# A two-layer graph kernel: some of layer 1's matrix products, its PSUM tiles, its decode buffers and one early sum are placed elsewhere in the order of work

## The chip, the core and the metric

The kernel runs on one core of a Trainium2 chip. The metric is the device time of one execution in microseconds (us). Three executions of the kernel before took 404.49, 404.73 and 406.21 us; the median, 404.73 us, is the time before. A separate execution was recorded by the hardware profiler. The engines are named as in the profile: PE is the matrix engine (PEld its weight loads), DVE the vector engine, ACT the activation engine, POOL the general engine, SP the queue that issues most DMAs.

## The reference, cut to what matters

There are 3327 nodes with 64 features and a dense 0/1 adjacency matrix. Layer 0 is a hyperbolic graph layer: for every pair of nodes a weight (a sigmoid of two logits) times a distance function of the two feature vectors, summed over the neighbours. Layer 1 gives each neighbour j of node i a weight 0.5 to the power of the number of neighbours behind it in the row, for the last 100 of them, and sums:

```python
h = relu(layernorm(x)); x = x + layer0(h, adj)      # pairs, sums over neighbours, then work per node
h = relu(layernorm(x)); support = h @ weight
rank = cumsum(adj != 0, axis=1)
k = minimum(rank[:, -1:], 100); pos = rank - (rank[:, -1:] - k)
w = mask * where(pos > 0, 0.5 ** (k - pos), 0)
x = x + w @ support + bias
```

Layer 1's weights depend on the adjacency alone, so they can be made while layer 0 runs. Its products need the new h of every node j, and so the end of layer 0 for that node.

## The kernel before, in words

**Tiles and rounds.** Nodes are padded to 26 blocks of 128. Columns i are cut into four strips of 8, 8, 6 and 4 blocks (`STRIPS`). Within a strip the row blocks j run from 25 down to 0. A round is one row block (strips 0 to 2) or two (strip 3), so there are 26, 26, 26 and 13 rounds, R = 91 of them, numbered n = 0 to 90. The loop `for n in range(2, R)` (L1228) issues them; rounds 0 and 1 are written out ahead of it.

**What a round does.** `load` brings the adjacency tile four rounds ahead. `edges` (L621, DVE) makes a 0/1 mask. `count` (L632 and L633, PE) adds masks into the PSUM tile `pc`, and `read` (L650 on ACT, L652 or L654 on DVE) takes out of `pc` the count for layer 1: as bytes into `behind_lo` and `behind_hi`, or, for the four row blocks 12 to 15 (`JD`), at once as ready bf16 weights into the tile `weight_of`. `products` (L678 and L679, PE) makes the pair terms in a tile `pq` of two PSUM banks, two buffers of it. `gelus` (L870, L871, ACT) works on `pq`, `sigmoids` (L661, ACT) makes `sg`, `pair_one` (L666, DVE) multiplies `sg` by the adjacency, and `pair_two` (L671, DVE) reads `pq` and multiplies. `total` (L691, PE) sums `sg` over j into PSUM banks `po0` and `po1`; it runs two rounds later. Counting runs one round ahead of the pairs.

**Order.** PE, DVE and ACT run their instructions in the order in which the code issues them, each one waiting at the head of its queue. In round 2 the order on PE is: products of round 3, count of round 3, sums of round 1 (`total(1)`, L1269). Then follow, in round 3, products of round 4 and count of round 4.

**End of a strip.** `strip_out` (L1172, DVE) copies the sums, `turn` (L1184, PE) transposes them, `per_node` copies the result (L1194, DVE) and starts `post`: some 60 small steps per node that end with `s2` (L1162 on ACT, L1164 on DVE), the operand of layer 1's products. `post` is a generator; each round lets it go on by some portions (`advance`). For the last strip its steps run on DVE, three powers on POOL, and three steps on ACT.

**Layer 1.** `order` holds row blocks 12 to 15, 0 to 11 and 16 to 21; 22 to 25 are `late`, since they need the last strip's `s2`. For each j, `add` issues 7 products (chunks n = 0 to 6 of the 3328 columns) into seven PSUM tiles `pw`. `decode` turns the bytes of a row block into weights: 22 blocks, on ACT one instruction (L1311), on DVE two (L1314, L1315). In order of their calls the 1st, 4th, 7th and so on go to ACT (`ACT_DECODES = 3`), 8 in all, and 14 to DVE. They go into 7 buffers `wt`. At step i of the loop over `order`, decoding has been issued for the first i + 5 entries (`LEAD = 4`), then `post` is advanced by 8 portions, then the seven products of order[i] are issued. After the loop the late blocks follow chunk by chunk (L1380), each chunk being copied out (L1358 to L1362) and multiplied by the layer's weight matrix (L1370).

All seven `pw` tiles come from a PSUM pool that is opened after every pool of layer 0 is closed (L1321 to L1323).

Of the kernel before, what the change touches and what calls it, by code (L numbers as in the profile page):

```python
# [2 lines left out]

# [1 line left out]

# [6 lines left out]
F32 = mybir.dt.float32  # L12
# [27 lines left out]
BIG, LATER, ACT = 4, 99, 100  # L40
ROUND = (3.5, 3.5, 2.8, 1.9)

LEAD = 4
ACT_DECODES = 3

GSTRIPS = [(0, 7), (7, 7), (14, 6), (20, 6)]
GFMAX = 7 * P
# [400 lines left out]
def fast(ctx, tc, x, adj_t, r, w_att, b_att, weight, bias, out, flag):  # L448
# [223 lines left out]

    def products(n):
        S = strips[rounds[n][0]]
        pq_of[n] = pq = ps.tile([P, FMAX], F32, name="pq", bufs=2)
        for j in js(n):
            for f0, f1 in S.hv:
                T.matmul(part(n, pq, j, f0, f1), ju[:KB, j, :], S.iu[:, f0:f1], start=True, stop=False)  # L678
                T.matmul(part(n, pq, j, f0, f1), jz[:, j, :], S.iz[:, f0:f1], start=False, stop=True)  # L679
# [13 lines left out]

    sums, pairs = ctx.enter_context(ExitStack()), ctx.enter_context(ExitStack())
    ps = sums.enter_context(tc.tile_pool(name="ps", bufs=1, space=PSUM))
    of_first = sums.enter_context(ExitStack())
    first_ps = of_first.enter_context(tc.tile_pool(name="first_ps", bufs=1, space=PSUM))
    strip = pairs.enter_context(tc.tile_pool(name="strip", bufs=2))
    work = pairs.enter_context(tc.tile_pool(name="work", bufs=2))
# [136 lines left out]
    edges(0)  # L836

    iz, iu = strip_in(0)
    pt = ps.tile([P, 16, P], F16, name="pq", bufs=2)
    for b in range(8):  # L840
        T.transpose(pt[:KB, b, :], nui[:, b, :], id16)
    pz = ps.tile([P, 16, P], F16, name="pq", bufs=2)
    for b in range(8):
        T.transpose(pz[:, b, :], nzi[:, b].rearrange("p c d -> p (c d)"), id16)
    for b in (0, 1):
# [4 lines left out]
    V.tensor_copy(ju[: KB + 7, last_j], pt[: KB + 7, 8:10, :])  # L850
    A.copy(iz, pz[:, :8, :])
    A.copy(jz[:, last_j], pz[:, 8:10, :])
    p3 = ps.tile([P, 16, P], F16, name="pq", bufs=2)
    for to, of in ((jz[:D], iz[D:]), (jz[D:], iz[:D]), (ju[:D], iu[:D]), (ju[D : D + 3], iu[D + 3 : D + 6]),
                   (ju[D + 3 : D + 6], iu[D : D + 3]), (ju[KB : KB + 7], iu[D:])):
        nc.gpsimd.dma_start(to[:, first_i], of)
# [64 lines left out]
    gelus(1)  # L921
    logits((high,))
    pair_one(1)
    p5 = ps.tile([P, FMAX], F32, name="pq", bufs=2)
    p4 = p5.bitcast(F16).rearrange("p (b q) -> p b q", q=P)
    turned_to(p4, low, 0)
    kept(p4, low, 0)
# [250 lines left out]

    def turn(k):
        nb = STRIPS[k][1]  # L1180
        pa = [bank(n) for n in range(nb // per_bank(k))]
        for b in range(nb):
            n, c0 = b // per_bank(k), b % per_bank(k) * (D + 1)
            T.transpose(pa[n][:, c0 : c0 + D + 1], strips[k].ot[:, b * P : (b + 1) * P], ident[: D + 1, : D + 1])  # L1184
        return pa
# [32 lines left out]
    def finish():  # L1218
# [2 lines left out]
                pass  # L1221
        stages.clear()

    stages, rest_of_ahead = [Stage(range_steps())], last_of_ahead()
    range_end = in_range()
    load(LOADS)
    load(LOADS + 1)
    for n in range(2, R):  # L1228
        k, lo, hi = rounds[n]
        m, w = n + AHEAD, span(n)  # L1230
        ended, turned = (n > i and rounds[n - i - 1][1] == 0 for i in (1, 2))
        if n + LOADS < R:
            if rounds[n + LOADS][2] == NB:
                strip_in(rounds[n + LOADS][0])
            load(n + LOADS)
        fresh = EARLY <= m < R
        two = fresh and len(js(m)) == 2
        if two:
            count(m, js(m)[0])
        apart = k + 1 == len(STRIPS)  # L1240
        if turned and not apart:
            pa = turn(k - 1)
        if n >= 4 and (apart or not turned):
            total(n - 2)
        gelus(n)
        asked_of_act()
        if turned and not apart:
            finish()
            stages.append(Stage(per_node(k - 1, pa)))
        pair_one(n)  # L1250
        if two:
            read(m, js(m)[0])
        if EARLY <= m + 1 < R:
            edges(m + 1)
        if n == 2:
            for j in js(2):
                read(2, j, True)
        if n < 4:
            products(n + 1)
        if fresh:  # L1260
            count(m, js(m)[-1])
        if n + 1 < R:
            sigmoids(n + 1)
        if fresh:
            read(m, js(m)[-1])
        if 4 <= n < R - 1:
            products(n + 1)
        if n == 2:
            total(1)  # L1269
        if ended:  # L1270
            strip_out(k - 1)
        if hi - lo > 1:
            advance(PORTIONS[k])
        if turned and apart:
            pa = turn(k - 1)
        pair_two(n)
        if turned and apart:
            finish()
            stages.append(Stage(per_node(k - 1, pa)))
        if n < 4:  # L1280
            next(rest_of_ahead)
            continue
        advance(PORTIONS[k])
        if turned and not apart:
            total(n - 2)
        if n > R - 3:
            next(range_end)
    total(R - 2)
    total(R - 1)
    strip_out(len(STRIPS) - 1)  # L1290
    pa = turn(len(STRIPS) - 1)
    pairs.close()


    late = STRIPS[-1][0]
    order = [*JD, *range(JD.start), *range(JD.stop, late)]
    chunks = [(q, r) for q in range(3) for r in range(2)] + [(3, None)]
    widths = [512] * 6 + [256]
    with tc.tile_pool(name="l1", bufs=2, reuse_waits="tile") as l1, tc.manual_schedule(engines=IN_ORDER):
        decoded = 0  # L1300

        def decode(j):

            nonlocal decoded
            if j in JD:
                return behind(j)
            wt = l1.tile([P, NP], U16, name="wt", bufs=7)
            decoded += 1
            to = by_parity(wt)
            if decoded % ACT_DECODES == 1:  # L1310
                A.activation(to, behind(j).rearrange("p (k r) -> p r k", r=2), AF.Copy, scale=128.0)  # L1311
            else:
                pairs_of = behind(j).bitcast(U16)
                V.tensor_scalar(to[:, 0], pairs_of, 0xFF, 7, op0=ALU.bitwise_and, op1=ALU.logical_shift_left)  # L1314
                V.tensor_scalar(to[:, 1], pairs_of, 0xFF00, 1, op0=ALU.bitwise_and, op1=ALU.logical_shift_right)  # L1315
            return wt
# [1 line left out]
        every = [*order, *range(late, NB)]  # L1318
        weights = {j: decode(j) for j in every[: len(JD) + 1]}
        stages.append(Stage(per_node(len(STRIPS) - 1, pa)))  # L1320
        sums.close()  # L1321
        l1_ps = ctx.enter_context(tc.tile_pool(name="l1_ps", bufs=1, space=PSUM, reuse_waits="tile"))
        pw = [l1_ps.tile([P, f], F32, name=f"pw{n}") for n, f in enumerate(widths)]  # L1323

        def add(j, wt, n):
            q, r = chunks[n]
            w = by_parity(wt.bitcast(BF16))[:, :, 512 * q : min(512 * q + 512, NP // 2)]
            T.matmul(pw[n], s2[:, j].rearrange("p c d -> p (c d)"), w if r is None else w[:, r],  # L1328
                     start=j == order[0], stop=j == NB - 1)

        def bias(b0, nb):
            xb = x_sb[:, b0 : b0 + nb]
# [2 lines left out]
        for i, j in enumerate(order):  # L1335
# [3 lines left out]
            asked_of_act()  # L1339
            advance(LAST)  # L1340
            for n in range(len(chunks)):
                add(j, weights[j], n)
            if i % 4 == 3 and i < STRIPS[-2][0]:
                bias(i - 3, 4)
        finish()
# [8 lines left out]
        def copied(n):  # L1354
            q, r = chunks[n]
            to = kept_of[q].rearrange("p (k r) -> p r k", r=2)
            if r is None:
                V.tensor_copy(to, by_parity(pw[n]))  # L1358
            elif r == 0:
                V.tensor_copy(to[:, 0], pw[n])  # L1360
            else:
                A.copy(to[:, 1], pw[n])  # L1362
# [75 lines left out]
```

## Time and profile before

| | us |
|---|---|
| median of three executions | 404.73 |
| the profiled execution, whole | 406.06 |
| its span from the first to the last instruction | 404.3 |
| DVE, ACT, PE busy in the span | 366.7, 355.8, 353.7 |
| POOL busy | 117.7 |
| layer 1's products, first to last of those in the loop | 354.11 to about 385.3 |

All times in the text are places in the profiled execution, counted from the start of its span, unless they are called the time or the median. The profiled execution is 1.76 us longer than its span, and 1.33 us longer than the median. A row of the timeline gives start, duration, engine, line, operation, output and inputs, and in brackets the idle time ahead of it with what ended it. The duration of a pipelined instruction reaches into that of the next one: a run of 138 products over 28.03 us gives one each 0.203 us, though each is written as some 0.36 us long.

### The profile page before, as it was taken

The numbers are of one execution on the slowest core, as the hardware profiler recorded it, in microseconds if no ns is written. First come the engines' busy times: TensorE is split into PE (matmuls) and PEld (weight loads), VectorE is DVE, ScalarE is ACT, GpSimd is POOL, SyncE is SP. The second block draws the span as 40 slices with busy tenths as digits, with TensorE's granted clock in tenths as the row PEclk, the third lists the DMA queues.
The fourth block names the chain that finished last, engine by engine and source line by source line (L and its number), as shares of the span: only waits on it lengthen the run. The fifth ranks groups of instructions, "written<-read, shape, count | busy, mean of one in ns | idle before, by whom it ended". The sixth has DMA issues, their size and how long they took to land.

```text
span 404.3 us, 4738 instructions
## 1 busy us (share of the span) xinstructions
PE 353.7 (87%) x1460; PEld 150.3 (37%) x1460; DVE 366.7 (91%) x563; ACT 355.8 (88%) x407; POOL 117.7 (29%) x240
## 2 busy tenths in 40 slices
PE   0077899999999899999999899999979899899992
PEld 0053333333333333333333444444433333254462
DVE  3999899999999989999999999899999999899831
ACT  3589999999999899999999999999998999858710
POOL 8145200000000053870052052850240767241200
PEclk9999999999999899999999999999999999999997
DMA  7314545454547434543434435444563340000012
GB/s 208 142 42 133 170 144 154 131 159 148 160 146 229 152 107 156 156 155 107 153 115 149 149 119 156 133 139 120 158 191 106 114 148 0 0 2 1 2 39 54
DMA packets 23298, 48.99 MB, mean 121 GB/s; under 512 B 8789, under 2 KB 9245, under 8 KB 23265
## 3 DMA queue, kind: packets, MB, share of 16 engines
q1 hardware_dynamic: 20993, 47.66, 38.1%
q10 hardware_dynamic: 1808, 0.46, 0.6%
q0 software_dynamic: 464, 0.49, 0.5%
q8 instruction: 13, 0.21, 0.2%
q14 instruction: 20, 0.16, 0.1%
HBM read 46.40 MB, written 0.87 MB: 117 GB/s over the span
## 4 chain that ended last, share of the span: by engine, by line
DVE 39%; PE 24%; ACT 23%; issue 10%; DMA 1%; DVEq 0%; ACTq 0%
DVE sg L671 13%; DVE sg L666 11%; PE pw L1328 9%; ACT pq L870 7%; ACT sg L661 7%; PE po L691 6%; DVE behind_lo L654 3%; ACT pq L871 3%; ACT behind_lo L650 2%; PE pq L678 2%; PE pq L679 2%; DVE behind_hi L654 2%; DVE mask L621 2%; PE pc L632 2%; PE pw L1370 2%
## 5 line engine op out<-in xcount | busy, mean ns | idle before, releaser
L691 PE MATMUL po<-sg,hw 128*65 128x512 f32 (+1 forms) x364 | 160.2, 563 | 0.4 <-DVE st L987 0.4
L671 DVE SCALAR_TENSOR_TENSOR sg<-pq,sg 128x1024 f32<-128x1024 f32 (+1 forms) x91 | 103.7, 1140 | 4.3 <-ACT pq L871 3.8
L666 DVE SCALAR_TENSOR_TENSOR sg<-sg,ad 128x1024 f32<-128x1024 f32 (+1 forms) x91 | 104.2, 1146 | 0.2
L661 ACT ACTIVATE sg<-left_b,right 128x1024 f32<-128x1024 f32 (+2 forms) x103 | 99.5, 978 | 0.0
L871 ACT ACTIVATE pq<-pq 128x1024 f32<-128x1024 f32 (+1 forms) x91 | 86.2, 947 | 2.9
L870 ACT ACTIVATE pq<-pq 128x1024 f32<-128x1024 f32 (+1 forms) x91 | 87.1, 957 | 1.6 <-PE pq L679 1.3
L691 PEld LDWEIGHTS po<-sg,hw 128*65 128x65 f32 x364 | 49.2, 138 | 68.9 <-issue 54.2
L632 PE MATMUL pc<-mask,ca 128*128 128x512 bf16 (+1 forms) x175 | 63.5, 363 | 11.0 <-ACT behind_hi L650 3.2
L678 PE MATMUL pq<-iu,ju 71*128 71x512 f16 (+1 forms) x182 | 67.0, 368 | 1.7 <-ACT jz L807 0.8
L633 PE MATMUL pc<-mask,cb 128*128 128x512 bf16 (+1 forms) x182 | 64.9, 367 | 2.7 <-ACT behind_lo L650 1.7
L679 PE MATMUL pq<-iz,jz 128*128 128x512 f16 (+1 forms) x182 | 65.5, 367 | 0.0
L621 DVE TENSOR_SCALAR mask<-ad 128x1024 bf16<-128x1024 f32 (+1 forms) x91 | 58.8, 647 | 0.0
L1059 POOL TENSOR_TENSOR dots<-dots,ih 128x8 f32<-128x8 f32 (+1 forms) x3 | 3.7, 1223 | 131.0 <-DVE dots L1079 131.0
L633 PEld LDWEIGHTS <-cb 128*128 128x128 bf16 x182 | 17.7, 97 | 52.2 <-issue 40.5
L1328 PE MATMUL pw<-wt,s 128*128 128x512 bf16 (+1 forms) x154 | 31.4, 364 | 0.0
L632 PEld LDWEIGHTS <-ca 128*128 128x128 bf16 x175 | 17.1, 98 | 30.3 <-issue 18.0
L678 PEld LDWEIGHTS <-ju 71*128 71x128 f16 x182 | 17.9, 98 | 23.6 <-DVE sg L671 5.9
L679 PEld LDWEIGHTS <-jz 128*128 128x128 f16 x182 | 18.0, 99 | 18.9 <-issue 2.0
L650 ACT ACTIVATE behind_lo<-pc 128x1024 uint8<-128x1024 f32 (+2 forms) x29 | 24.9, 859 | 0.0
L1328 PEld LDWEIGHTS <-s 128*128 128x128 f16 x182 | 17.8, 99 | 18.2
L1333 POOL TENSOR_TENSOR x_sb<-x_sb,bias_b 128x256 f32<-128x256 f32 (+1 forms) x6 | 8.3, 1394 | 51.9 <-DVE w L1148 46.0
L650 ACT ACTIVATE behind_hi<-pc 128x1024 uint8<-128x1024 f32 (+2 forms) x25 | 21.8, 871 | 1.6 <-PE pc L633 1.5
(318 smaller groups left out, 347.3 us busy)
## 6 DMA issues: line engine op xcount, KB each, us to landing
ad<-in_adj_t SPq DMA_DIRECT2D x65, 512.0 KB, 3.5
ad<-in_adj_t SPq DMA_DIRECT2D x26, 384.0 KB, 3.1
out<-o SPq DMA_DIRECT2D x6, 128.0 KB, 1.9
left_b<-left_d SPq DMA_DIRECT2D x1, 512.0 KB, 4.3
x_sb<-in_x ACTq DMA_DIRECT2D x1, 416.0 KB, 5.5
x_sb<-in_x SPq DMA_DIRECT2D x1, 416.0 KB
left_b<-left_d SPq DMA_DIRECT2D x1, 384.0 KB
jz<-iz POOLq DMA_DIRECT2D x2, 128.0 KB, 2.6
```

The source lines that it names most:

```text
L621: V.tensor_scalar(*args, 0.0, None, op0=ALU.not_equal)
L632: T.matmul(S.pc[:, f0:f1], ca, S.before[:, f0:f1], start=False, stop=True, skip_group_check=True)
L633: T.matmul(S.pc[:, f0:f1], cb, now[:, f0:f1], start=S.first, stop=True, skip_group_check=True)
L661: A.activation(part(n, sg, j), S.left[:, : S.F], AF.Tanh, bias=right[:, j : j + 1], scale=0.5)
L666: V.scalar_tensor_tensor(sg, sg, 1.0, ad_of.pop(n)[:, :w], op0=ALU.add, op1=ALU.mult)
L671: V.scalar_tensor_tensor(sg, pq_of.pop(n)[:, :w], WD, sg, op0=ALU.add, op1=ALU.mult)
L678: T.matmul(part(n, pq, j, f0, f1), ju[:KB, j, :], S.iu[:, f0:f1], start=True, stop=False)
L679: T.matmul(part(n, pq, j, f0, f1), jz[:, j, :], S.iz[:, f0:f1], start=False, stop=True)
L691: T.matmul(po[: D + 1, : f1 - f0], hw[:, j, :], part(n, sg_of[n], j, f0, f1), start=j == NB - 1, stop=j == 0)
L870: A.activation(pq, pq, AF.Gelu, scale=-WG / QS)
L871: A.activation(pq, pq, AF.Gelu, scale=WH)
L1328: T.matmul(pw[n], s2[:, j].rearrange("p c d -> p (c d)"), w if r is None else w[:, r], start=j == order[0], stop=j == NB - 1)
```

## The change

It does six things.

- In round 2, `total(1)` is issued ahead of count(3) in place of behind it.
- `pq` gets a PSUM pool of its own on the other side of PSUM; it is closed after the last round. Four `pw` tiles (chunks 1 to 4) take its four banks. Chunk 0 takes `po0`, chunk 5 `po1`, and chunk 6 the `pc` tile. The last `turn` uses the `pc` tile in place of `po0`.
- Chunk 0's products of the four `JD` row blocks are issued one each in rounds 87 to 90, at the end of the round.
- Of the 16 products of chunks 1 to 4 with these blocks, two are issued between `total(89)` and `total(90)`, four between the last `strip_out` and the last `turn`, ten ahead of the loop over `order`. Chunks 5 and 6 stay in it.
- `LEAD` is 7. Decodes go in turn into the 7 `wt` buffers and into the four places of `weight_of`, 11 in all.
- ACT takes two of five decodes: in order of their calls, numbers 3, 5, 8, 10, 13, 15, 18 and 20. These are 8 again, and DVE keeps 14.

```diff
-LEAD = 4
-ACT_DECODES = 3
+LEAD = 7
+BESIDE, GAPS = (1, 2, 3, 4), (2, 4)
+ACT_DECODES = (2, 5)
...
-        pq_of[n] = pq = ps.tile([P, FMAX], F32, name="pq", bufs=2)
+        pq_of[n] = pq = pq_ps.tile([P, FMAX], F32, name="pq")
...
+    pq_ps = of_pq.enter_context(tc.tile_pool(name="pq_ps", bufs=2, space=PSUM, side="right"))
...
-        pa = [bank(n) for n in range(nb // per_bank(k))]
+        pa = [bank(n) for n in range(nb // per_bank(k))] if k + 1 < len(STRIPS) else [ps.tile([P, FMAX], F32, name="pc")]
...
             products(n + 1)
+        if n == 2:
+            total(1)
         if fresh:
             count(m, js(m)[-1])
...
-        if n == 2:
-            total(1)
...
+        if n >= R - len(JD):
+            if n == R - len(JD):
+                pw[0] = bank(0)
+            add(JD[n - R], behind(JD[n - R]), 0)
         if n > R - 3:
             next(range_end)
+    of_pq.close()
+    l1_ps = ctx.enter_context(tc.tile_pool(name="l1_ps", bufs=1, space=PSUM, side="right", reuse_waits="tile"))
+    for n in BESIDE:
+        pw[n] = l1_ps.tile([P, 512], F32, name=f"pw{n}")
+    beside = iter([(n, j) for n in BESIDE for j in JD])
     total(R - 2)
+    for n, j in islice(beside, GAPS[0]):
+        add(j, behind(j), n)
     total(R - 1)
     strip_out(len(STRIPS) - 1)
+    pw[5] = bank(1)
+    for n, j in islice(beside, GAPS[1]):
+        add(j, behind(j), n)
     pa = turn(len(STRIPS) - 1)
...
-            wt = l1.tile([P, NP], U16, name="wt", bufs=7)
+            spare = decoded % (7 + len(JD)) - 7
+            wt = weight_of[:, spare] if spare >= 0 else l1.tile([P, NP], U16, name="wt", bufs=7)
             decoded += 1
             to = by_parity(wt)
-            if decoded % ACT_DECODES == 1:
+            if decoded * ACT_DECODES[0] % ACT_DECODES[1] < ACT_DECODES[0]:
...
-        sums.close()
-        l1_ps = ctx.enter_context(tc.tile_pool(name="l1_ps", bufs=1, space=PSUM, reuse_waits="tile"))
-        pw = [l1_ps.tile([P, f], F32, name=f"pw{n}") for n, f in enumerate(widths)]
+        pw[6] = ps.tile([P, FMAX], F32, name="pc")
+        for n, j in beside:
+            add(j, behind(j), n)
...
             for n in range(len(chunks)):
-                add(j, weights[j], n)
+                if j not in JD or n > 4:
+                    add(j, weights[j], n)
```

## The prediction

> **What bounds the kernel now.** I read the busy tenths first.
>
> ```profile
> PE   0077899999999899999999899999979899899992
> ...
> DVE  3999899999999989999999999899999999899831
> ACT  3589999999999899999999999999998999858710
> ...
> PEclk9999999999999899999999999999999999999997
> ```
>
> PE, DVE and ACT are all full through layer 0: a place is worth only what the engine that ends last there gives. Two stretches are touched: slice 4, counted from 0 (40 to 50 us), where DVE shows an 8, and the last six (from 344 us), where ACT falls off, then DVE, and PE stays at 8 and 9 nearly to the end. In slice 13 (131 to 142 us) PE's clock drops. Next the timeline of rounds 2 and 3.
>
> ```profile
> 41.44 1.02 ACT L650 ACTIVATE behind_hi<-pc 128x1024 uint8<-128x1024 f32 x1
> ...
> 42.51 0.38 PE L632 MATMUL pc<-mask,ca 128*128 128x512 bf16 x1 [1.29 <-ACT behind_hi L650]
> ...
> 43.37 1.88 PE L691 MATMUL po<-sg,hw 128*65 128x512 f32 x4
> ...
> 47.10 1.23 DVE L654 TENSOR_SCALAR behind_hi<-pc 128x1024 uint8<-128x1024 f32 x1 [1.73 <-PE pc L633]
> ```
>
> PE stands 1.29 us before count(3), because ACT still reads `pc`; sums of round 1 follow it. DVE then stands 1.73 us for count(4). Then the timeline of the end, with the chain of waits beside it (the chain's last pieces are the DVE pair at 349.82, the sums on PE at 351.12, and PE's layer-1 products from 354.27 to the end).
>
> ```profile
> 351.10 1.93 PE L691 MATMUL po<-sg,hw 128*65 128x512 f32 x4 [0.44 <-DVE st L987]
> ...
> 353.07 0.69 DVE L1172 COPY sg<-po 65x512 f32<-65x512 f32 x1 [1.19 <-PE po L691]
> ...
> 353.81 0.46 PE L1184 MATMUL po<-ident,sg 65*128 65x65 f32 x4 [0.78 <-DVE sg L1172]
> ...
> 354.11 5.78 PE L1328 MATMUL pw<-weight_of,s 128*128 128x512 bf16 x28
> ...
> 359.73 28.03 PE L1328 MATMUL pw<-wt,s 128*128 128x512 bf16 x138
> ...
> 381.82 0.42 DVE L1164 TENSOR_TENSOR s<-w_last,s 128x256 f16<-128x256 f32 x1
> ```
>
> From 354.11 on PE is the bound: 166 products without a gap. 126 of the 138 belong to the loop, so the first late product comes at 359.73 + 126 x 0.203 = 385.3. The last strip's `s2` is ready at 382.24, 3.1 us earlier. This slack is the second clock of the end.
>
> **Part 1, total(1) ahead of count(3).** No instruction is added. Products(3) end issue at 41.07 (last start 40.85 + 0.22). total(1) takes 1.72 (43.37 to 45.09), so it runs 41.07 to 42.79, mostly in the idle 1.29; its inputs were ready at 37.4. Count(3) starts at 42.79, not 42.51: **0.28 later**. Behind it ACT's read(3) ends at 44.88 (was 44.59), PE's products(4) at 44.53 (was 45.97). Count(4) waits for that read: 44.93, was 45.97. DVE's read(4), the instruction that waits 1.73, moves from 47.10 to 46.06: **1.04 earlier** on DVE and PE, while ACT is 0.29 later.
>
> Does 1.04 last? To 132 us DVE has no wait, and its `pair_two` runs behind ACT by 2.7 us in round 9 and by 1.5 in round 25 (70.10 against 67.36, 127.91 against about 126.4), so ACT can be 1.04 nearer. At 131.92 DVE's strip copy releases PE:
>
> ```profile
> 132.65 0.72 PE L1184 MATMUL po<-ident,sg 65*128 65x65 f32 x8 [1.84 <-DVE sg L1172]
> ...
> 134.00:135.00 1.00, 1.00 (x4) 0.30 (x2) 1.00 (x2) 1.00 (x2) 0.00 (x0) 0.50 0.00 0
> ```
>
> In this execution the matrix clock was 0.50 (third number from the end) from 133.9 to 137.1, which loses about 1.6 us of PE's work; PE then sets the pace to 159, ACT waiting 1.53 + 0.29 at 141 and 145. Here the whole **1.04** passes on. In an execution without that stretch those ACT waits shrink to about 0.3, and from 145 to 298 ACT is full. ACT by itself is 0.29 late but drops two waits for PE (0.45 at 68.8, 0.22 at 75.9): about 0.4 earlier, and up to 0.7 with what is left at 145. I take **0.65** there.
>
> Which execution is the median? The Trainium skill, "TensorE: Matmul & The Clock Gate", Part 1 (the HAM clock gate), says that PE falls to half rate after an idle window of about 3.4 us, free-running against the kernel. By the rule taken as a gap of 3.4 us, an idle of 1.84 would never do it; the row shows that it did. By the rule no execution has the stretch and I would subtract 0.65 from any; by the row it comes or not with the window's phase, which fits 404.49 and 404.73 against 406.21, with 406.06 for the profiled one. So I take the median as one without it: 1.33 below the profiled execution.
>
> **Part 2, the ten products ahead of 353.8.** No product is added; ten of 28 leave the gapless run: 10 x 0.203 = **2.03** on PE. *In rounds 87 to 90*: one product, 0.21, behind products(n+1). PE has about 0.3 there (products end 342.69, the next count starts 343.00, waiting for ACT): hidden. In round 90 it is ahead of L985, which starts at 348.64: 0.1 later, ahead of a wait. Without cover each costs 0.21. *Two between total(89) and total(90)*: total(89) ends issue at about 350.5, total(90) waits to 351.10: 0.41 into 0.6. *Four* (0.83) between 352.8 and 353.81: fit.
>
> The new wait is on PSUM: `pw1` lies on a `pq` buffer. If it is that of round 90, the two products wait for `pair_two(90)` (to 351.04), and total(90) is queued behind them. No row shows it. Bounds: nothing (other buffer), or 2 x 0.206 = 0.41 for total(90) and DVE's `strip_out` behind it. The same page, Part 2 ("Step-by-step"), speaks against the change here: matmuls stay in program order, only weight loads are pulled ahead. By that, a blocked product costs its 0.41; by the 0.6 of idle in the row, nothing. Buffers alternate and I can't tell which; I take 0.1. `pw6` waits for `agg`'s copy (355.1), and is first used at about 356.5; `pw5` for `strip_out`: nothing.
>
> **Part 3, decodes.** 8 on ACT and 14 on DVE as before (2.97, and 2 x 0.505). What changes is DVE's order against the post steps, by the code's portions. Decode 1 is now on DVE, between `strip_out` and the copy of `agg`: 353.70 to 354.71, while the copy could start at 354.31: +0.40. From there to L1164 DVE does 13 decodes, as before (numbers 2, 4, 6, 7, 9, 11, 12, 14, 16, 17, 19, 21, 22; earlier 2, 3, 5, 6, 8, 9, 11, 12, 14, 15, 17, 18, 20). But the second and third POOL power, out and back in about 1.7, had two decodes (2.01) over them and now have one: about 0.69 each, +1.4. The square at 376.69 had 0.48 uncovered and gets decode 19: -0.48. The tanh on ACT may stand behind decode 10: +0.2. Sum +1.5, so `s2` at 383.75. ACT's last steps (tanh, square, cast) each wait behind a 2.97 decode if one has just begun; by my order of ACT's queue the square and the cast don't. As the gaps are rough I put the sum at +1.2 to +1.5: `s2` at about **383.6**.
>
> Buffers: ACT's waits of 0.63 and 1.23 (for `wt`) go, off the path. Decodes 8 to 11 write `weight_of` after its products are done (by 358).
>
> **The end together.** PE reaches the late blocks at 385.3 - 2.03 = 383.3, and finds `s2` at 383.6: the late wait is new, and DVE's chain with ACT and POOL is next. With 0.1 for PSUM: 383.7, so **1.6** gained; the 19.0 us behind it are unchanged.
>
> Sum against the profiled execution: 406.06 - 1.04 - 1.6 = 403.4 with the clock stretch. Against the median: 404.73 - 0.65 - 1.6 = 402.5.
>
> **Rivals.**
> *A, as forecast:* both parts. 402.5 (402.0 to 402.9, and down to 401.7 if all 1.04 and all 2.03 count). 0.57.
> *B, the early part gives nothing or the clock stretch is in the median execution:* ACT is full from 42 to 298 and starts 0.29 late; 404.73 - 1.6 = 403.1, or 403.4. For it: ACT's row of nines. Against: its two removable waits. 0.24.
> *C, the gaps don't pay:* the two products wait for `pair_two(90)` (0.41), and one ACT step stands 1.0 behind a decode: `s2` at 385.0, so only 0.3 at the end; 404.73 - 0.65 - 0.3 = 403.8. For it: one engine queue in order. Against: ACT has idle time between decodes. 0.14.
> *D, slower:* ACT's decodes stand ahead of tanh, square and cast of the last strip, which hold DVE's queue. Price up to 2.97 at each of three. It decides once the chain is over 3.1 + 0.65 = 3.7 longer than before; two full hits on top of 1.2 give 7.1 and 404.73 - 0.65 + 4.0 = 408.1. Against: before, decodes 7, 10, 16 and 19 stood near the same steps with 0.5 waited at most. 0.05.
>
> **Numbers.** Predicted 402.5. Range 401.5 to 404.0: A with its bounds, B, and most of C. About 0.5% (2.0 us, 402.7) is what a measurement of this kernel can tell from no change. Faster by more: most of A and some outcomes of B with 0.2 less, 0.58. Within: 0.38. Slower: 0.04 (D, less its mild end).
>
> **What would show it.** Right: total(1) starting near 41.1 with count(3) directly behind; read(4) on DVE near 46.1; DVE's strip copy near 130.9; 18 `weight_of` products in the gapless run in place of 28; a new wait of PE for L1164 or L1162 of under 0.6 ahead of the late products. Wrong: DVE waiting for ACT's L871 before 130; total(90) starting at 351.5 less the early gain (C); ACT's tanh, square or cast waiting behind L1311 (D).

## The result and the profile after

The changed kernel takes 404.21 us (median of 22 executions, 401.58 to 405.79) against 405.87 us of the kernel before (22 executions, 404.40 to 408.03). The ratio is 0.9961, 95% interval 0.9947 to 0.9975: some 1.6 us faster (1.0 to 2.1), within the 0.5% that the prediction called no change. The forecast of 402.5 lies 1.7 us below it, and the range ended 0.2 below it at 404.0. As a step, the forecast had 2.2 (404.73 to 402.5), and the medians show 1.7. The profiled executions took 406.06 and 404.32 us.

The busy tenths of the changed kernel, whose slices are 10.06 us long:

```profile
PE   0087999999999999999999899999979899999992
...
DVE  4989999999999989999999999899999999898941
ACT  3589999999999999999999999999998999869510
...
PEclk9999999999999899999999999999999999999997
```

In these tenths the picture is nearly the old one. DVE's slice 4 is full now. The clock has its dip in slice 13 again, and at the end ACT falls off, then DVE, and PE is last. What changed is inside the slices.

**Rounds 2 and 3.** The timeline of the changed kernel (lines 635, 656 and 693 here are 633, 654 and 691 of before):

```profile
41.11 1.88 PE L693 MATMUL po<-sg,hw 128*65 128x512 f32 x4
...
42.82 0.38 PE L634 MATMUL pc<-mask,ca 128*128 128x512 bf16 x1
...
43.89 1.02 ACT L652 ACTIVATE behind_hi<-pc 128x1024 uint8<-128x1024 f32 x1 [0.35 <-PE pc L635]
...
46.09 1.22 DVE L656 TENSOR_SCALAR behind_hi<-pc 128x1024 uint8<-128x1024 f32 x1 [0.67 <-PE pc L635]
```

The sums of round 1 fill the 1.29 us in which PE stood, count(3) follows directly, and DVE's read, the instruction that waited 1.73, waits 0.67 and starts 1.01 earlier. ACT pays 0.35. Neither DVE nor ACT has another wait worth the name from there to the turn at 131.

**The first strip's turn.** The timeline's line of the turn, and the stretches behind it, of the changed kernel (third number from the end: PE's clock):

```profile
131.65 0.81 PE L1187 MATMUL po<-ident,sg 65*128 65x65 f32 x8 [1.68 <-DVE sg L1175]
```

```profile
132.00:133.00 1.00, 1.00 (x8) 0.56 (x7) 1.00 (x3) 0.97 (x2) 0.00 (x0) 0.55 0.19 74
133.00:134.00 1.00, 1.00 (x4) 0.34 (x3) 1.00 (x2) 1.00 (x3) 0.00 (x0) 0.50 0.00 0
...
135.00:136.00 1.00, 1.00 (x4) 0.37 (x2) 1.00 (x2) 1.00 (x2) 0.00 (x0) 0.74 0.67 111
```

The turn is 1.00 earlier than before (132.65). Both profiled executions have the half clock (a granted clock of 0.50) behind it: from 133.9 before, from 132.1 here. The gain is still 1.03 at the last strip's copy (353.07 before, 352.04 here).

**The end.** The timeline of the changed kernel from the last sums on:

```profile
349.69 0.59 PE L1237 MATMUL pw<-weight_of,s 128*128 128x512 bf16 x2
...
350.12 1.89 PE L693 MATMUL po<-sg,hw 128*65 128x512 f32 x4
...
351.84 1.03 PE L1237 MATMUL pw<-weight_of,s 128*128 128x512 bf16 x4
...
352.04 0.69 DVE L1175 COPY sg<-po 65x512 f32<-65x512 f32 x1 [1.19 <-PE po L693]
...
352.78 0.46 PE L1187 MATMUL pc<-ident,sg 65*128 65x65 f32 x4
...
353.08 2.32 PE L1237 MATMUL pw<-weight_of,s 128*128 128x512 bf16 x10
...
353.65 0.42 DVE L1197 COPY agg_last<-pc 128x260 f32<-128x260 f32 x1
...
355.24 0.38 PE L1237 MATMUL po<-weight_of,s 128*128 128x512 bf16 x1
355.46 0.27 PE L1237 MATMUL pc<-weight_of,s 128*128 128x256 bf16 x1
355.57 0.38 PE L1237 MATMUL po<-weight_of,s 128*128 128x512 bf16 x1
```

The two and the four products lie in PE's gaps; the sums behind the two start 0.98 earlier than before (351.10), so the gap hides them and nothing waits for `pw1`. The last rows size a product: ten take 355.24 - 353.08 = 2.16, which is 0.216 each, and the seventh chunk of a row block, 256 columns wide, takes 0.11. A row block of the loop then takes 6 x 0.216 + 0.11 = 1.41. Before, the loop's products began at 354.11 with 28, and by these sizes the first late product came at 359.73 + 18 x 1.41, which is about 385.0 and not 385.3, with no wait ahead of it. After:

```profile
371.04 0.16 DVE L1062 TENSOR_TENSOR rt_last<-rn_last 128x4 f32<-128x4 f32 x1 [0.40 <-POOL rn_last L1062]
...
376.74 1.01 POOL L1352 TENSOR_TENSOR x_sb<-x_sb,bias_b 128x256 f32<-128x256 f32 x1 [5.73 <-DVE w_last L1151]
...
377.08 1.12 DVE L1340 TENSOR_SCALAR weight_of<-behind_hi 128x1664 uint16<-128x1664 uint16 x1
...
380.14 0.16 DVE L1062 TENSOR_TENSOR rt_last<-rn_last 128x4 f32<-128x4 f32 x1 [0.41 <-POOL rn_last L1062]
...
382.28 0.42 DVE L1167 TENSOR_TENSOR s<-w_last,s 128x256 f16<-128x256 f32 x1
...
382.75 1.04 PE L1237 MATMUL po<-weight_of,s 128*128 128x512 bf16 x4 [0.77 <-DVE s L1167]
```

PE is through the loop and stands 0.77 for `s2`, which is ready at 382.70. The first late product comes some 2.2 earlier than before: 1.03 from the early part, 1.2 from the end. ScalarE's last DMA issue follows at 395.34, was 397.58. Behind it some 7.3 us pass to the end of the span, where the first profile of before has some 6.7 and every other profile of this study 7.1 to 7.5; so that pair of executions differs by 1.74 and not by 2.24.

### The profile page after: what moved, and what is told of

Same layout as the page of the kernel before. It is cut to its first block, busy times and chain, and to the rows that moved or that the text cites. A ratio compares the mean times of both kernels' runs of the same rounds, so it can differ in the third digit from the quotient of the medians.

```text
span 402.6 us, 4731 instructions
## 1 busy us (share of the span) xinstructions
PE 355.0 (88%) x1460; PEld 151.9 (38%) x1460; DVE 367.3 (91%) x563; ACT 355.3 (88%) x407; POOL 118.1 (29%) x240
## 4 chain that ended last, share of the span: by engine, by line
DVE 32%; ACT 32%; PE 19%; issue 12%; DMA 1%; POOL 1%; POOLq 0%; DVEq 0%; ACTq 0%
ACT sg L663 11%; ACT pq L873 9%; DVE sg L673 8%; DVE sg L668 7%; PE po L693 7%; ACT behind_lo L652 3%; ACT pq L874 3%; PE pc L635 2%; PE pc L634 2%; PE pq L680 2%; PE pq L681 2%; ACT weight_of L652 2%; DVE behind_hi L656 2%; DVE mask L623 1%; ACT behind_hi L652 1%
## 5 line engine op out<-in xcount | busy, mean ns | idle before, releaser
L844 PE MATMUL pq<-id,nui 128*71 128x128 f16 x8 | 1.0, 311 | 21.2 <-ACT nzi L818 21.2
```

## Experiments

A short key: in every profile I read three places, the start of the first turn on PE, the last strip's copy (352.04 above), and ScalarE's last DMA issue. "Tail" is the time from the second to the third. "Half clock at" leaves out the end of the span, where PE has little or no work left and each profile has it. The ratio is the recorded estimate; it is not the quotient of the two medians and differs from that by up to 0.002.

| kernel | median us (executions) | ratio to before | half clock at | first turn | turn to last copy | tail |
|---|---|---|---|---|---|---|
| before, first profile | 405.87 (22) | 1 | 134 | 132.65 | 220.42 | 44.51 |
| before, again | 404.86 (1) | | 40 | 132.69 | 218.72 | 44.51 |
| the change, first profile | 404.21 (22) | 0.9961 | 132 | 131.65 | 220.39 | 43.30 |
| the change, again (1) | 402.19 (1) | | 32 | 131.10 | 218.91 | 43.27 |
| the change, again (2) | 404.15 (1) | | 133 | 131.60 | 220.34 | 43.26 |
| the change, again (3) | 404.50 (1) | | 133 | 131.61 | 220.39 | 43.27 |
| early sum alone | 405.73 (14) | 0.9999 | 32 | 131.57 | 219.01 | 44.50 |
| end alone | 403.70 (9) | 0.9953 | none | 133.13 | 218.67 | 43.26 |
| change + count ahead of the turn | 402.91 (6) | 0.9930 | none | 131.83 | 218.77 | 43.25 |
| before + count ahead | 404.72 (22) | 0.9975 | 40 | 133.17 | 218.19 | 44.51 |
| early sum + count ahead | 404.41 (22) | 0.9982 | 40 and 296 | 133.58 | 220.06 | 44.50 |
| change, other ACT decodes | 404.27 (16) | 0.9958 | 132 | 131.58 | 220.36 | 43.14 |
| change, old decode order | 403.74 (11) | 0.9960 | 32 | 131.17 | 218.94 | 43.12 |
| other ACT decodes + count ahead | 402.85 (22) | 0.9938 | 32 | 131.25 | 218.68 | 43.16 |
| the same + fill at 293 | 403.84 (17) | 0.9959 | 32 | 131.39 | 218.79 | 43.18 |
| change + count ahead + fill at 293 | 403.22 (7) | 0.9937 | 296 | 131.72 | 219.57 | 43.29 |
| before + count ahead + fill at 293 | 405.49 (14) | 1.0001 | 40 | 132.90 | 218.14 | 44.51 |
| change + count ahead, last decode order | 402.87 (15) | 0.9937 | none | 131.91 | 218.65 | 42.35 |

Two things stand in it. The tail is 44.5 in each kernel with before's end and 43.1 to 43.3 with the change's. And the time from the turn to the last copy is 220.3 to 220.4 with the half clock behind the turn and 218.1 to 219.0 without (the two others, 220.06 and 219.57, have it at 296). So the place of the half clock in a profile tells the time from the turn to the copy, and the kernel's form tells the tail.

**The two parts alone.** The early sum in the kernel before:

```diff
             products(n + 1)
+        if n == 2:
+            total(1)
         if fresh:
             count(m, js(m)[-1])
...
-        if n == 2:
-            total(1)
```

> The kernel before with one edit: total(1) of round 2 ahead of count(3). Theory (the two parts of the change add up, and the half-clock stretch of PE's clock near 132 us comes or not in either kernel): read(4) on DVE near 46.1, DVE's last strip copy near 352.0 in an execution with the stretch (was 353.07), the rest of the end unchanged with 0 wait for s2; 1.0 us faster in executions with the stretch, 0.65 in those without, ratio about 0.998. Rival (ACT, which starts 0.29 late, sets the pace, so that the early part is worth nothing): strip copy at 352.9 or later, 0 to 0.2 us faster, ratio 0.9995 or more.

Measured: ratio 0.9999 (0.9980 to 1.0019). Its profiled execution, 403.99 us with the half clock at 32, has the turn at 131.57 and the last copy at 350.58; before, again, with it at 40, has 132.69 and 351.41. So the early us is there in the trace and absent from the time: the 0.998 that was expected lies at the edge of the interval, and the rival's "0.9995 or more" fits, though not its strip copy at 352.9 or later. Its times have a gap between 404.50 and 405.38, with 9 of 14 executions above it; those of before beside them have theirs between 405.49 and 405.83, with 13 of 32 above.

The change with that edit taken back:

```diff
             products(n + 1)
-        if n == 2:
-            total(1)
         if fresh:
             count(m, js(m)[-1])
...
+        if n == 2:
+            total(1)
```

> The changed kernel with total(1) back behind count(3), so the end part alone. Theory: last strip copy near 353.1 as before, the first late product about 383.8 (was 384.96), with a wait of PE for s2 of about 0.8; 1.2 us faster than before less what the very end takes, ratio about 0.997. Rival (the decode order on DVE eats the ten products): first late product later than 384.5, 0 to 0.4 us faster, ratio 0.999 or more.

Measured: 0.9953 (0.9937 to 0.9970), tail 43.26. The end is worth 44.51 - 43.26 = 1.25 us, by the trace; its median lies 1.55 below that of the kernel before beside it (405.25). With 0.9953 it is no slower than the whole change with 0.9961.

**The half clock behind the turn.** In the change, the count that follows the turn is put ahead of it, so that PE has work in the 1.7 us:

```diff
         if turned and not apart:
+            count(m, js(m)[-1])
             pa = turn(k - 1)
...
-        if fresh:
+        if fresh and (apart or not turned):
             count(m, js(m)[-1])
```

> The changed kernel, and in the round where a strip is turned, the count of the next round is issued ahead of the turn on PE in place of behind it. Theory (the half-clock stretch comes from PE standing about 1.9 us for the strip copy near 131): the stand splits, 0.9 of it is filled, PE's clock stays at 1.00 from 130 to 140, and the executions lie close together near 402.0 to 402.5, ratio to before about 0.991. Rival 1 (the stretch doesn't come from this stand): PE's clock still falls in the profile or the executions spread over 3 us or more as the changed kernel's do. Rival 2 (the stretch costs nothing because ACT sets the pace): no stretch, but the time no better than 0.5 us below the changed kernel.

Measured: 402.91 us, ratio 0.9930 (0.9912 to 0.9949), its six executions within 0.22 us. The timeline of this kernel:

```profile
129.52 0.38 PE L681 MATMUL pq<-iz,jz 128*128 128x512 f16 x1
130.97 0.38 PE L634 MATMUL pc<-mask,ca 128*128 128x512 bf16 x1 [1.07 <-DVE behind_hi L656]
...
131.83 0.66 PE L1187 MATMUL po<-ident,sg 65*128 65x65 f32 x8
```

PE stands 1.07 in place of 1.68, the turn comes 0.2 later than in the change, and no row behind it is below 1.00 until the end. Its median is 1.3 us below that of the change, but the two intervals overlap, and the 402.0 to 402.5 expected was not reached. Six executions are few, so I put the same edit on the kernel before, on the early sum alone, and on the change with the next decode pattern.

> The kernel before, with the count of the next round issued ahead of the turn of a strip on PE. So neither part of the change, and the stand of PE near 131 filled. Theory: no half-clock stretch near 132, executions close together near the lower group of before, 404.6 to 405.3 with a median near 405.0; last strip copy near 351.9. Rival (the spread of before has another cause): executions still spread over 2 us or more.

> The same with total(1) ahead of count(3) too. Theory: with the stretch out of the way the early sum is worth its 1.0: median 1.0 to 1.2 below that of the kernel with the count alone (near 404.0), last strip copy near 350.7, and the remaining 1.1 to the kernel with everything and the count ahead (402.9) is the end part. Rival (ACT's 0.29 takes the early gain): 0 to 0.5 below.

> The changed kernel with the count ahead of the turn and the other choice of ACT's decodes (numbers 1, 3, 5, 8, 10, 13, 16 and 18). Theory: both gains add, executions close together near 402.4 (402.9 with the count alone, 0.5 from the decodes), ratio to before about 0.992. Rival (PE's end is bound by something else than s2): no better than 402.9.

Measured: 0.9975 (0.9960 to 0.9989), 0.9982 (0.9966 to 0.9998) and 0.9938 (0.9923 to 0.9953). With the edit, most executions of each lie close together (18 of 22 between 404.22 and 405.17; 15 of 22 between 403.06 and 404.87; 17 of 22 between 401.62 and 403.19), where only 6 of the change's 22 lie in its lowest group. The medians fall by 0.8 us against the kernel before beside it (405.49), and by 1.3 and 1.4 against the same kernels without the count; only the first of these three, 0.9975, is clear of noise against its partner. Two expectations missed: the early sum was to be worth 1.0 to 1.2 us once the stretch was gone, and the second median is only 0.3 below the first, with the worse ratio; and the third was to come to 402.4 and is no better than the change with the count alone.

What is left above can have another place, which the profiled execution of the second (407.14 us) shows. Its timeline, and its stretches:

```profile
295.14 0.38 PE L633 MATMUL pc<-mask,cb 128*128 128x512 bf16 x1 [1.74 <-ACT behind_lo L650]
```

```profile
39.00:40.00 1.00, 1.00 (x5) 0.33 (x4) 1.00 (x2) 0.76 (x2) 0.00 (x0) 0.82 0.75 177
...
295.00:296.00 1.00, 0.86 (x3) 0.35 (x3) 1.00 (x2) 0.97 (x3) 1.00 (x1) 0.82 0.57 106
296.00:297.00 1.00, 1.00 (x3) 0.38 (x2) 1.00 (x3) 1.00 (x2) 0.69 (x4) 0.50 0.96 371
```

A stand of 1.74 us at the start of the fourth strip, and half clock behind it: the same thing at a second place. I tried to fill that stand too, with the sums of round 75 put ahead of the first count, in three kernels:

```diff
         two = fresh and len(js(m)) == 2
+        apart = k + 1 == len(STRIPS)
+        if two and not apart:
+            total(n - 2)
         if two:
             count(m, js(m)[0])
...
-        if n >= 4 and (apart or not turned):
+        if n >= 4 and (apart or not turned and not two):
```

> The changed kernel with the count ahead of the turn, the other ACT decodes, and in round 77 the sums of round 75 ahead of the first count of strip 3, where PE stands 1.7 us near 293 waiting for ACT's last read of strip 2. Theory (a second half-clock stretch near 296, after that stand, makes the executions above 404 us; the profile of the kernel with the early sum and the count shows one, in an execution of 407): no execution above 403.5, median near 402.5, ratio to before about 0.991. Rival (the slow executions come from elsewhere): a quarter of the executions above 404 as without this edit.

> The changed kernel with both stands filled (count ahead of the turn, sums of round 75 ahead of the count) and its own decodes. Theory: median near 402.9, no execution above 403.6.

> The kernel before with both stands filled. Theory: the worth of the change with the stretches out of the way is 2.0 to 2.3 us, so this one's median is 404.9 to 405.2 against 402.9, and its executions lie within 1.2 us. Rival (the change is worth only the 1.6 that the medians show): 404.4 to 404.6.

Measured: 0.9959 (0.9945 to 0.9973), 0.9937 (0.9913 to 0.9961) and 1.0001 (0.9985 to 1.0017): no gain in any of them (the medians are 0.3 to 1.0 us above those of the same kernels without the fill), their executions spread over 2.1 to 2.8 us, where at most 1.2 was expected of the third, and the second has the half clock at 296 all the same. The timeline of the first says why:

```profile
294.79 0.38 PE L634 MATMUL pc<-mask,ca 128*128 128x512 bf16 x1 [1.44 <-DVE behind_hi L656]
```

The stand was moved to the next count, which waits for DVE, and not filled. So these kernels don't show what a filled stand at 293 would be worth.

**Which executions have it.** The change, and before, once more:

> The changed kernel again, one look. Theory: an execution near 402.4 shows no stretch at 132 and at 296, one near 404 shows one of them, one near 405.5 both. Rival: the time doesn't follow these two places.

> The change once more, one look. Theory (the place of the half-clock rows sets the execution's time): with rows at 0.5 in 132 to 136 the last strip copy is near 352.0 and the time near 404.3; with none there, nor in 290 to 300, 350.0 and 402.2; with both 353 to 355 and over 405. Rival (the groups come from something else, as DMA landing late at the start): the last strip copy lies at another place than the half-clock rows say by over 0.5 us.

> The change once more, one look; the same as for the look before it: 404.3 us with half-clock rows in 132 to 136, 402.2 without, over 405 with rows at 290 to 300 as well; the rival sees the last strip copy over 0.5 us away from what the rows say.

> The kernel before once more, one look. Theory: with half-clock rows in 132 to 137 the last strip copy is at 353.1 and the time near 406.5, as ScalarE's last DMA issue is followed by some 7.2 us instead of the 6.7 of its first profile; without such rows 351.8 and near 405.0. Rival (its end is really shorter by half a us than the change's): 6.7 us again behind that issue.

Measured: 402.19, 404.15, 404.50 and 404.86 us. The first of them has its half clock elsewhere; its turn, and the stretches of it there and behind the turn:

```profile
131.10 0.71 PE L1187 MATMUL po<-ident,sg 65*128 65x65 f32 x8 [1.71 <-DVE sg L1175]
```

```profile
32.00:33.00 1.00, 1.00 (x15) 0.50 (x13) 1.00 (x2) 0.97 (x2) 1.00 (x3) 0.50 0.69 111
...
133.00:134.00 1.00, 1.00 (x5) 0.45 (x4) 1.00 (x2) 1.00 (x2) 0.00 (x0) 1.00 0.00 0
```

It stands 1.71 before the turn, as the others do, and keeps its clock. The place of the half clock went with the time in all four, to within 0.4 us of what was expected: 352 at the last copy and 404.2 to 404.5 us with it behind the turn, 350.0 and 402.2 without it, 351.4 and 404.9 for before without it. Before without it is 218.72 from turn to last copy, with it 220.42: it costs **1.7** there, and 220.37 - 218.91 = **1.5** in the change (mean of three against one). At 32 or 40 it leaves the time from the turn to the copy as it is. Before has some 7.2 behind the last issue here, so the 6.7 of its first profile belongs to that execution.

The traces also tell where the half clock can begin. A row's mean clock gives the moment: 0.55 in 132.00 to 133.00 of the change's first profile is a begin at 132.10, and with 0.74 in 135.00 to 136.00 it ends at 135.52, so it lasts 3.42 us. The 0.82 twice in the profile of the early sum with the count are begins at 39.64 and 295.64, and 256.00 between them is 75 times 3.413. Fifteen profiles have two begins or more, with the one at the end of the span, and each of the sixteen distances is a whole multiple of 3.413 to within 0.02 us. So each execution has marks 3.413 us apart at which the clock is set, and their place differs from execution to execution. Counted from a begin in the same profile (for the end alone, the one at 395.8), the marks around the stand ahead of the first turn, in the ten profiles without the count ahead of it, are:

| profile | PE stands | marks | half clock behind the turn |
|---|---|---|---|
| before, first | 130.81 to 132.65 | 130.46, 133.87 | yes |
| the change, first | 129.97 to 131.65 | 128.69, 132.10 | yes |
| the change, again (2) | 129.91 to 131.60 | 128.80, 132.21 | yes |
| the change, again (3) | 129.95 to 131.61 | 129.53, 132.94 | yes |
| change, other ACT decodes | 129.87 to 131.58 | 129.12, 132.53 | yes |
| before, again | 130.87 to 132.69 | 131.66 | no |
| the change, again (1) | 129.39 to 131.10 | 130.26 | no |
| early sum alone | 129.90 to 131.57 | 130.97 | no |
| end alone | 131.30 to 133.13 | 132.96 | no |
| change, old decode order | 129.48 to 131.17 | 130.69 | no |

Where the stand lies whole between two marks, the half clock begins at the second of them; where a mark cuts the stand, the clock stays. So the place of the marks is what parts the executions here, of the same kernel too. This was read off after the runs, and no run moved the marks. It also isn't all: the stand of 1.7 us near 293 lies whole between two marks in eleven profiles, and only the one of 407.14 us has the half clock behind it; why is open. The count ahead of the turn does more than luck: in two of its profiles (the change with the count and the fill, and the last kernel below) the shorter stand of 1.07 and 1.10 lies whole between two marks, and the clock stays.

**The decode order at the end.** In the change, ACT's eight decodes get other places; in a second kernel, the old order comes back with the 11 buffers kept:

```diff
-ACT_DECODES = (2, 5)
+ACT_DECODES = (1, 3, 5, 8, 10, 13, 16, 18)
...
-            if decoded * ACT_DECODES[0] % ACT_DECODES[1] < ACT_DECODES[0]:
+            if decoded in ACT_DECODES:
```

> The changed kernel with other decodes on ACT: numbers 1, 3, 5, 8, 10, 13, 16 and 18. So the copy of agg has no decode ahead of it, and both the second and the third power have two decodes over them. Theory (the new wait of 0.8 at the late products is the chain on DVE, and its waits for the two powers, 0.40 and 0.41, and the decode ahead of agg's copy, 0.37, are what made it): s2 about 0.2 to 0.8 earlier in spite of one more decode on DVE, PE's wait for it 0.1 to 0.6, time 0.3 to 0.7 below the changed kernel. Rival (the chain is bound by DVE's sum of work and the waits only fill it): s2 0.3 or more later, PE's wait 1.0 or more, time 0.3 above the changed kernel.

```diff
-LEAD = 7
+LEAD = 4
...
-            if decoded * ACT_DECODES[0] % ACT_DECODES[1] < ACT_DECODES[0]:
+            if decoded % 3 == 1:
```

> The changed kernel with the old decode order: LEAD 4 and every third decode on ACT, in 11 buffers. Only the products and their tiles are changed. Theory (the new wait for s2 is made by the decode order): s2 comes 1.2 to 1.5 earlier against the last strip copy (29.2 behind its start in place of 30.7), so PE's wait at the late products for s2 is gone; PE may wait up to 0.6 for the last decode instead; time 0.2 to 0.8 below the changed kernel at equal strip copy. Rival (the old order starves PE, now that PE starts 2.1 earlier): PE waits for wt in the loop, time equal to the changed kernel or above.

Measured: tails of 43.14 and 43.12, against 43.30 of the change; 404.27 us (0.9958, 0.9938 to 0.9977) and 403.74 us (0.9960, 0.9936 to 0.9984), in which the groups of executions hide a gain of this size. In the first, `s2` is ready 30.50 behind the last copy, 0.16 earlier than in the change, less than the 0.2 to 0.8 expected. In the second, `s2` is ready 29.17 after the last copy, as before, and not 30.66. But the late products then wait for something else; PE's timeline of it:

```profile
379.88 0.81 PE L1237 MATMUL po<-weight_of,s 128*128 128x512 bf16 x3
381.31 0.38 PE L1237 MATMUL po<-weight_of,s 128*128 128x512 bf16 x1 [0.61 <-ACT weight_of L1336]
```

The last decode, number 22, is ACT's in the old order, 2.97 long, and begins behind ACT's last step of `post`. So the last kernel keeps the old lead, gives number 22 to DVE and has ACT take number 2, with the count ahead of the turn. Against the kernel with other ACT decodes and that count:

```diff
-LEAD = 7
+LEAD = 4
...
-ACT_DECODES = (1, 3, 5, 8, 10, 13, 16, 18)
+ACT_DECODES = (1, 2, 4, 7, 10, 13, 16, 19)
```

> The change, with the sums of a third strip counted ahead of the turn, the old decode lead (4 instead of 7) and decodes 1, 2, 4, 7, 10, 13, 16 and 19 of 22 on ScalarE, so that the last one is VectorE's. Theory (the end is short by the waits that the decode order leaves): no TensorE wait of over 0.2 us for the transposed sums and none for the last decode, 42.6 us from the last strip copy to ScalarE's last DMA issue (43.30 in the change, 43.12 with the old order alone), 402.2 us. Rival (VectorE and ScalarE together are what the end is short of, and any order leaves some wait): 43.1 us or more for that stretch, one of the two waits at 0.5 us or more, 402.8 us.

Measured: tail 42.35, shorter than the theory's 42.6. Its timeline:

```profile
378.76 0.42 DVE L1167 TENSOR_TENSOR s<-w_last,s 128x256 f16<-128x256 f32 x1
...
380.23 0.27 PE L1237 MATMUL pc<-wt,s 128*128 128x256 bf16 x1
380.34 1.03 PE L1237 MATMUL po<-weight_of,s 128*128 128x512 bf16 x4
```

`s2` is ready over 1 us ahead of PE, PE goes from the loop into the late blocks without a wait, and all of the ten products' 2.16 us arrive: 44.51 - 42.35 = 2.16. The median is 402.87, ratio 0.9937 (0.9913 to 0.9960): 9 of 15 executions lie between 401.41 and 402.88 and 6 between 404.36 and 405.21. The interval lies below 1, and the fastest execution of the study (401.41) is among them. But the 402.2 expected did not come: against the change with the count alone (402.91) the medians are the same; the 0.9 us of the shorter tail are in the trace, and the time shows them only in the lower group.

The upper group was not profiled in this kernel, but the mean granted clock of each execution is on record. All six have 0.985: 2 x 0.015 x 403 = 12.1 us at half clock. The end of the span takes 4.0 to 7.1 of that in the profiles, and one stretch 3.41, so these executions have more than one stretch ahead of the end. Where is not recorded.

## Why the prediction was wrong, point by point

**The early part: right in place and size in the trace.** total(1) at 41.11 (forecast 41.07), count(3) at 42.82 (42.79), the read on DVE at 46.09 (46.06), ACT 0.35 late (0.29), and 1.03 at the last copy where 1.04 was to pass on with the half clock in both. Without it in either, the forecast was 0.65; 351.41 against 350.01 in the executions of 404.86 and 402.19 us is 1.40. Two single executions do not size this better than "1.0 or a little more".

**The end: right in mechanism, 0.4 too large.** The ten products left the gapless run (forecast 2.03, measured 2.16), the in-gap products were hidden, PE's new wait for DVE is there, and the chain of DVE grew by 30.66 - 29.17 = 1.49, which is the upper end of the forecast +1.2 to +1.5. The mis-sized term is the slack: "the first late product comes at 359.73 + 126 x 0.203 = 385.3". The mean of 0.203 came from a run that ends with 12 of the late blocks' wide products and counts the last one at its whole written length. The loop has a half-width product in every seven, 1.41 / 7 = 0.201 on average: 385.0, and a slack of 385.0 - 382.24, about 2.8 instead of 3.1. So the end gained some 2.8 - 1.5 = 1.3 by these sums, 1.21 to 1.25 by the tails, and not 1.6. Inside the 1.49 the terms were less good than their sum: the two waits for POOL's powers are 0.40 and 0.41 (forecast 0.69 each), and the decode that was to fill 0.48 of idle gained nothing, because one half of it took 1.12 in place of 0.58 beside POOL's addition of the bias.

**The failing step: "So I take the median as one without it."** For the median I took three executions, two at 404.5 to 404.7 and one at 406.2, as two without the half clock behind the turn and one with it. The reading of the groups held: executions profiled without it took about 404.9 and 402.2, those with it 406.1 and 404.3. The choice did not. Over 22 executions the medians are 405.87 and 404.21. Of before, 13 of 22 lie at 405.54 or above. Of the change only 6 lie at 401.58 to 402.51, the group that the forecast 402.5 describes; 8 lie at 403.46 to 404.35, where two profiles (404.15 and 404.32) show the half clock behind the turn, with a third just above (404.50); and 8 at 404.79 to 405.79, which no profile of the change caught. Six of these 8 have a mean granted clock of 0.983 or 0.984, which by the sum under the last experiment is more than one stretch.

In numbers: the forecast is 404.73 - 2.25 and the result 405.87 - 1.66. So 1.1 of the miss of 1.7 is the time that was subtracted from, and 0.6 the gain. The first part is in part the luck of three executions: before was timed in five sets of 20 to 64 executions, and their medians run from 404.91 to 405.87. Of the gain, the end was sized 0.4 too large, and the 0.65 of the early part did not reach the time: 0.9999 alone, 0.9982 against 0.9975 with the count, and the change no better than the end alone. The interval of the gain, 1.0 to 2.1 us, is too wide to share the 0.6 out between them.

Rival B (0.24) named both: "the early part gives nothing or the clock stretch is in the median execution". Its reason for the first, an ACT that is full and starts 0.29 late, is refuted by the traces, where 1.03 is still there at the last copy; its 403.1 and 403.4 stand on the same 404.73 and are too low too.

The rule of the Trainium skill ("TensorE: Matmul & The Clock Gate", Part 1, on the HAM clock gate) was weighed against the row there: half rate follows an idle window of about 3.4 us, free-running against the kernel. The traces agree with the window's length and with its running free: begins whole multiples of 3.413 apart, in another place in each execution. They do not agree that the window has to be idle: PE stood 1.66 to 1.84 of the 3.41 ahead of the half clock behind the turn. I used "free-running" to call the executions different and then treated the split of three as if it were the rate. An estimate from the rows: if the marks fall anywhere alike, a stand of 1.67 lies whole between two of them in (3.41 - 1.67) / 3.41 = 0.51 of the executions, one of 1.84 in 0.46. That is close to a coin, so the median can fall on either side.

**Rivals C and D: refuted.** total(90) starts 0.98 earlier, ahead of the forecast's own 0.1 for it, and of ACT's steps in `post` only the tanh stood behind a decode (its input was ready at 364.03, it began at 365.04), for which DVE waited 0.22: the +0.2 of the forecast. C had put a full us on such a stand.

**What stays open.** Why the early sum gives nothing to its own median. Divide each kernel's times at its gap (403 for the change and the decode orders, 405 for the early sum alone; the times of before have no clean gap near 405.5). Of the kernels with the early sum and without the count ahead of the turn (the change, the early sum alone, the two decode orders) 43 of 63 executions lie above it, of before, over all sets, some 75 of 169. By the granted clock, at 0.985 or below, 17 of the 63 have more than one stretch ahead of the end by the same sum, and 11 of the 147 of before whose clock is on record. So the early sum may make stretches of half clock more frequent elsewhere; no run shows where, or why. A stretch at 32 or 40 goes with none at 132 because of the marks: 29 or 27 of them further on, one falls into the stand ahead of the turn (130.26 and 131.66 above).

## What to carry to other kernels

When executions of one kernel fall into groups, find in the trace what divides them before choosing the one to forecast, and count the groups over more than three executions: here the division was worth 1.7 us, as much as the change. A gain that is there in a trace need not reach the median; measure each part alone. Filling PE's stand (1.7 us ahead of the turn, with a count that was due anyway) lowered four medians by 0.8 to 1.4 us, not far from the edit under study, though only one of the four pairs is clear of noise by itself. A slack is a difference of two times, so size the run that ends it by its own shapes, not by a mean over a run that has others in it.

## What the runs showed that I had not expected

PE's clock fell to half for 3.4 us, in some executions, at four places: 32, 40, 132 and 296. At 132 PE had stood 1.66 to 1.84 us in one piece, at 296 1.74 (1.44 and 0.45 with the fill); at 32 two stands of 0.95 and 0.83 lie in the 3.41 ahead, at 40 two of 0.91 and 0.40. At 132 it cost 1.5 to 1.7, at 32 and 40 nothing behind the turn.

DVE's half decode (128x1664 uint16) takes 0.58 alone and 1.11 to 1.12 beside POOL's addition of 128x256 numbers, which itself takes 1.00 to 1.01 in place of 0.72 to 0.73: in each of the ten profiles with a decode there (the change four times, and six variants), and in none of those without (before, the old order, the last kernel). The Trainium skill, "GPSIMD Engine Reference", "Key points", has the two engines share their way to SBUF in some modes of DVE; the rows agree with that and do not show the mode.
